# One portion of column copies behind each Relu and each square, in a graph layer on one core

## The chip, the cores and the metric

The kernel runs on one core of one Trainium2 chip. The time is the device time of one execution, in microseconds (us), of the core's whole program. A core has four engines that compute (TensorE or PE, VectorE or DVE, ScalarE or ACT, GpSimd or POOL), and SyncE (SP) beside them, whose queue here issues nearly all the DMAs. Each engine carries out its own list of instructions in order, and the engines wait for each other by semaphores. The kernel's lists are unrolled: there is no loop in the fast path, and an order in the code is an order on the engine.

## The reference: what is computed

A layer of a graph network over 12,500 nodes of 96 features and 412,500 edges (both directions of 200,000 random pairs, and a loop at each node), sorted by target node:

```python
def _mlp(h, W, b, gamma, beta):
    h = jax.nn.relu(h @ W + b)
    mu = jnp.mean(h, axis=0)
    var = jnp.mean(jnp.square(h - mu), axis=0)
    return gamma * (h - mu) * jax.lax.rsqrt(var + EPS) + beta

node_feat = _mlp(x, W_node, ...)                       # 12500 x 96
edge_feat = _mlp(edge_attr, W_edge, ...)               # 412500 x 96, from 4 numbers an edge
message = concatenate([x[src], x[dst], edge_feat])     # 412500 x 288
message = _mlp(message, W_msg, ...)                    # 412500 x 96
agg = segment_sum(message, dst, 12500)
out = layernorm(x + agg + node_feat)                   # over the features
```

The mean and the variance run over all nodes or all edges, in float32. An edge's message is a Relu of three parts: a product of the source's features, one of the target's, one of the edge's features.

## The kernel before, in words

**Before the main loop.** `tables` multiplies x (which lies in SBUF, features on the partitions, in `xp`, the first 96 partitions of `big`) with two thirds of `W_msg`, and writes the rows to two tables in DRAM: `p_tab` by source node, `q_tab` by target node. `edge_norm` then runs over all the edges for the statistics of the edge features: in 26 turns it loads eight blocks of 2048 edges (`ea`), multiplies (L425), applies the Relu on ACT (L429) and takes the statistics on DVE (L431, `estats`). A loop in `fast` steps through it and in each turn also takes two steps of `nodes`, one of `early_rows`, and some of `store`. `nodes` makes the node features into `agg` (L370 to L372), normalises them and adds x (L381, L382; the result goes over x in `xp`), multiplies the result with a centering matrix (L398), and stores it as `y0` in DRAM (L400, L389). At its end it clears `agg` (L406), the place where the messages are summed later. Since x is gone by then, `back` loads it again from DRAM, in 14 DMAs on SP's queue (L498).

**The main loop** runs over 806 groups of 512 edges (four tiles of 128), one group a step `k`; four groups are a block. Source rows of `p_tab` are fetched by POOL, one indirect DMA for 128 rows (`gather`, L215). 116 early groups are fetched before the loop and parked in DRAM (`spill`); the other 690 are late groups, whose rows POOL brings into a ring of 16 groups while the loop runs. `plan` mixes the early blocks into the late ones. One step does, for its group or for neighbouring ones:

- `message(k)`, DVE (L741): h = Relu(z + source rows), where z is a product in PSUM;
- `squared`, ACT (L755): the squares of two groups of h, every second step;
- `moments`, DVE (L761): two additions of such squares to a sum in PSUM (`mixed`), every second step;
- `places_of`, DVE (L749), and `add`, DVE (L804, L805): once a block, which edge belongs to which node of a window, and the block's sums added to `agg`;
- `sums(k-2)`, PE (L785): the sums by node of the group two steps back;
- `edges`, PE (L705), and `prepare`, ACT (L713): half a block of edge features into the PSUM tile `pr`, of which there is one, and its Relu into `left`;
- `linear(k+2)`, PE (L721): z for the group two steps ahead, from `left` and `rhs` (weights and target rows).

**Column copies.** In every second late group, for three of four pairs, the fourth tile's source rows are not gathered by POOL. Its 128 columns of x are copied instead, one by one, from `xp` in SBUF into a tile `xc`, and multiplied by the source weights within `linear` (L726). There are 249 such tiles. A copy moves 96 x 4 bytes from a place that is only known at run time, so its engine first loads the places into registers: a load of numbers (`TENSOR_LOAD`, L644) brings a portion's places at once, and then a register instruction and a copy follow for each column (L655 on DVE, L657 on ACT). Two `Stream`s, one an engine, hand out portions of `AT_A_TIME` = 16 columns; `SHARES` gives ACT the first 64 or 80 columns of a tile and DVE the others. In each step a stream's credit grows by `RATE` times its portions a tile, and portions are issued while it lasts, as long as the tile's use is no more than `AHEAD_BY` steps away. Before a portion's copies stands the load of the portion after it:

```python
val = self.next or places_at(j, lo, hi, self.engine)
...
    self.next = places_at(*self.parts[self.done], self.engine)
columns(j, lo, val, self.engine)
```

On SP and POOL, and in the main loop on PE, DVE and ACT too, the instructions stand as the code writes them; before the loop a scheduler orders PE, DVE and ACT.

## Time and profile before

| | us |
|---|---|
| median of 3 runs (4052.61 to 4059.76) | 4056.29 |
| the profiled execution's own time | 4053.38 |
| its span in the profile | 4051.7 |
| busy: PE / DVE / ACT / POOL | 2504 / 3050 / 2998 / 2851 |
| first message of the main loop | at 708 |
| last gather issued by POOL | at 4002 |

In the profile's rows an engine's name with a q is its queue (ACTq, DVEq): the part that reads instructions and loads registers. Its time is not in the busy time. A group's row gives line, engine, operation, output and input, count, busy time and mean time in ns of one, then the idle time of the engine just before these instructions and what ended most of it; "issue" means that the engine waited for nothing that the profile shows. In rows in order of time, the first number is the start, the second the length from the first start to the last end of the merged instructions, and the bracket the idle time before. In the row of a window the columns are the window, its length, then for PE, weight loads, DVE, ACT and POOL the busy time and count, then the granted clock, the DMA engines' share, and GB/s.

### The profile page before, as it was taken

The numbers are of one execution on the slowest core, as the hardware profiler recorded it, in microseconds if no ns is written. First come the engines' busy times: TensorE is split into PE (matmuls) and PEld (weight loads), VectorE is DVE, ScalarE is ACT, GpSimd is POOL, SyncE is SP. The second block draws the span as 40 slices with busy tenths as digits, with TensorE's granted clock in tenths as the row PEclk, the third lists the DMA queues.
The fourth block names the chain that finished last, engine by engine and source line by source line (L and its number), as shares of the span: only waits on it lengthen the run. The fifth ranks groups of instructions, "written<-read, shape, count | busy, mean of one in ns | idle before, by whom it ended". The sixth has DMA issues, their size and how long they took to land.

```text
span 4051.7 us, 110364 instructions
## 1 busy us (share of the span) xinstructions
PE 2504.0 (62%) x15667; PEld 2145.1 (53%) x15667; DVE 3049.6 (75%) x16338; ACT 2997.5 (74%) x19818; POOL 2851.2 (70%) x2999
## 2 busy tenths in 40 slices
PE   3345554766666666666666666665666666566567
PEld 3012311665565566666556565555655565556557
DVE  2499898777777777777777777777777777777776
ACT  0465674778777787877787778778787777788774
POOL 7776676777766676767767667666776766767765
PEclk7666776778777777777877777878777877777778
DMA  8764574222222222222222222222222222222224
GB/s 222 270 158 109 149 189 101 57 61 60 55 55 47 54 57 57 58 55 59 57 55 57 57 58 46 55 58 56 57 56 56 60 54 57 57 45 66 48 56 122
DMA packets 209657, 314.64 MB, mean 78 GB/s; under 512 B 122822, under 2 KB 129716, under 8 KB 206080
## 3 DMA queue, kind: packets, MB, share of 16 engines
q0 software_dynamic: 95072, 146.22, 17.9%
q1 hardware_dynamic: 100876, 156.32, 12.9%
q10 hardware_dynamic: 12960, 4.93, 0.5%
q14 instruction: 623, 5.10, 0.4%
q8 instruction: 126, 2.06, 0.2%
HBM read 251.14 MB, written 56.09 MB: 76 GB/s over the span
## 4 chain that ended last, share of the span: by engine, by line
ACT 35%; DVE 19%; issue 18%; ACTq 12%; PE 6%; DMA 5%; DVEq 3%; SPq 1%; POOL 0%; POOLq 0%
ACT xc L657 32%; ACTq L644 10%; DVE estats L431 7%; DVE xc L655 5%; DVEq L644 3%; DVE mixed L761 2%; PE z L721 2%; ACTq L657 2%; DVE h L741 2%; ACT left L713 1%; DMA ea<-stack_d 1%; ACT sq L755 1%; PE pr L705 1%; PE pa L785 1%; DMA q_tab<-trow 1%
## 5 line engine op out<-in xcount | busy, mean ns | idle before, releaser
L215 POOL DMA_INDIRECT pg<-p_tab,src x2907 | 2768.2, 952 | 1151.1 <-issue 790.0
L657 ACT ACTIVATE xc<-big 96x4 uint8 x18592 | 1925.9, 190 | 626.1 <-issue 597.3
L655 DVE COPY xc<-big 96x4 uint8 x13280 | 1503.0, 198 | 696.9 <-issue 693.7
L721 PEld LDWEIGHTS z<-rhs,left 128*128 128x128 f32 x6446 | 1126.4, 254 | 219.0 <-DVE h L741 133.6
L721 PE MATMUL z<-rhs,left 128*128 128x96 f32 x6446 | 1159.5, 338 | 89.1 <-DVE h L741 88.2
L705 PE MATMUL pr<-late,we 128*128 128x512 bf16 x690 | 276.7, 493 | 933.0 <-ACT left L713 913.0
L785 PE MATMUL pa<-at,h 128*97 128x80 f32 x6446 | 837.7, 284 | 0.0
L785 PEld LDWEIGHTS pa<-at,h 128*97 128x97 f32 x6446 | 791.8, 205 | 0.2
L705 PEld LDWEIGHTS <-we 128*128 128x128 bf16 x806 | 86.4, 109 | 1097.7 <-issue 1096.9
L761 DVE TENSOR_TENSOR mixed<-mixed,sq 128x384 f32<-128x384 f32 x802 | 449.9, 561 | 16.3 <-ACT sq L755 2.2
L741 DVE CUSTOM_DVE_ANT_0 h<-z,pg 128x384 f32<-128x384 f32 x690 | 381.1, 556 | 76.8 <-PE z L721 52.1
L713 ACT ACTIVATE left<-pr 127x1024 f32<-127x1024 f32 x403 | 403.7, 1002 | 33.9 <-PE pr L705 33.9
L429 ACT ACTIVATE r<-pr 128x1024 f32<-128x1024 f32 x303 | 299.2, 1034 | 131.5 <-PE pr L425 68.6
L431 DVE BATCH_NORM_STATS2 estats<-r 128x6 f32<-128x512 f32 x606 | 361.3, 674 | 15.9 <-ACT r L429 15.9
L755 ACT ACTIVATE sq<-h 128x768 f32<-128x768 f32 x404 | 335.0, 829 | 43.0 <-DVE h L741 40.9
L425 PE MATMUL pr<-ea,wide 128*128 128x512 bf16 x606 | 225.7, 483 | 222.8 <-ACT r L429 111.8
L425 PEld LDWEIGHTS <-wide 128*128 128x128 bf16 x606 | 69.1, 115 | 367.6 <-issue 330.2
L749 DVE TENSOR_TENSOR at<-rel,mixed 128x496 f32<-128x496 bf16 x202 | 135.2, 669 | 6.8
L726 PE MATMUL z<-w_msg,xc 96*128 96x96 f32 x498 | 133.7, 364 | 0.0
L705 PE MATMUL pr<-early,we 128*128 128x512 bf16 x116 | 46.5, 493 | 117.3 <-ACT left L713 117.3
L726 PEld LDWEIGHTS z<-w_msg,xc 96*128 96x128 f32 x498 | 112.2, 277 | 0.0
L215 POOL DMA_INDIRECT pg<-in_x,src_raw x64 | 61.3, 957 | 20.7 <-issue 19.2
(131 smaller groups left out, 794.4 us busy)
## 6 DMA issues: line engine op xcount, KB each, us to landing
pg<-p_tab,src POOLq DMA_INDIRECT x2907
pb<-spill SPq DMA_DIRECT2D x29, 768.0 KB
spill<-pg SPq DMA_DIRECT2D x55, 384.0 KB
ea<-stack_d SPq DMA_DIRECT2D x25, 480.0 KB
stack_d<-y SPq DMA_DIRECT2D x24, 448.0 KB
late<-stack_d SPq DMA_DIRECT2D x57, 180.0 KB
big<-in_xp SPq DMA_DIRECT2D x28, 336.0 KB
rhs<-q_tab SPq DMA_DIRECT2D x202, 46.5 KB
```

Source lines behind the costliest of these rows:

```text
L215: made = [nc.gpsimd.indirect_dma_start(out=pg[:, i, :], out_offset=None, in_=tab[:, :], in_offset=bass.IndirectOffsetOnAxis(ap=idx[:, i:i ...
L431: nc.vector.bn_stats(stats[:, (k - o) % NS, (k - o) // NS, :], r[:, 1 - o, :])
L644: _, val = nc.values_load_multi_w_load_instructions(numbers[q // TURN % 2][:, q % TURN, lo:hi], engines=[engine], min_val=0, max_val=4 * ( ...
L655: nc.vector.tensor_copy(a, b)
L657: nc.scalar.activation(a, b, AF.Copy)
L705: nc.tensor.matmul(prs[s, half][:, i, :], we[:, 2 * half + i, :], block[s], start=True, stop=True)
L713: nc.scalar.activation(x[:C + WN, 2 * half:2 * half + n, :], pr[:C + WN, :n, :], AF.Relu)
L721: nc.tensor.matmul(zb[k % ZB][:, i * C:(i + 1) * C], left[s % 2][:KR, g % BG, i * P:(i + 1) * P], rhs[:KR, s % RB, g % BG, :], start=True, ...
L741: nc.vector._custom_dve(TENSOR_ADD_SAT, out=h[:, :n, :], in0=z, in1=rows[:, :n, :], s0=MOST, s1=0.0)
L755: nc.scalar.activation(sq[:, :m, :n, :], hb[k // 2 % HP][:, k % 2:k % 2 + m, :n, :C], AF.Square)
L761: nc.vector.tensor_tensor(wide_sq, wide_sq, sq[:, i, :, :], op=OP.add)
L785: nc.tensor.matmul(by_place[s % 2][:C + 1, :NW], hb[k // 2 % HP][:r, k % 2, t, :], at[s % AB][:r, i, o + NW * t:o + NW * (t + 1)], start=i ...
```

## The change

- **Portions.** `SHARES` now holds cuts: ACT's portions are columns 0 to 24, 24 to 48 and 48 to 72 of every tile, DVE's 72 to 92, 92 to 112 and 112 to 128. A load of numbers thus brings 24 places on ACT, and 20, 20 and 16 on DVE. `RATE` is 0.335, which with three portions a tile is one portion a step for each engine, and `AHEAD_BY` is 18.
- **Turns.** `squared` stands in even steps and takes the pair of groups before the current one; `prepare` stands in odd steps. `moments` moves to the even steps. `edges` stands in even steps, `transposed` in odd ones.
- **PE.** `linear(k+2)` comes ahead of `edges` in a step.
- **x.** The normalised nodes are written over `agg`, x stays in `xp`, and `back` with its 14 DMAs is gone. `nodes` takes one step a turn of `edge_norm` instead of two. The columns of `agg` past the last node are cleared at the start, since a product reads them.

```diff
-AT_A_TIME = 16
-SHARES = (64, 80, 80)
-AHEAD_BY = 12
-RATE = 0.36
+SHARES = ((0, 24, 48, 72), (72, 92, 112, P))
+AHEAD_BY = 18
+RATE = 0.335
@@ nodes
+        nc.vector.memset(agg[:C, N:], 0.0)
@@
-            x, y = agg[:C, c:c + N // 10], xp[:, c:c + N // 10]
-            nc.vector.scalar_tensor_tensor(y, x, a_n, y, op0=OP.mult, op1=OP.add)
+            y = agg[:C, c:c + N // 10]
+            nc.vector.scalar_tensor_tensor(y, y, a_n, xp[:, c:c + N // 10], op0=OP.mult, op1=OP.add)
@@
-                    nc.tensor.matmul(py[:, g * C:(g + 1) * C], xp[:, (i + o + g) * P:(i + o + g + 1) * P], center,
+                    nc.tensor.matmul(py[:, g * C:(g + 1) * C], agg[:C, (i + o + g) * P:(i + o + g + 1) * P], center,
@@ fast, the turns of edge_norm
-                    for _ in range(2):
-                        next(node, None)
+                    next(node, None)
@@
-                    if i > 14:
-                        for _ in range(min(3, len(homes))):
-                            back(homes.pop(0))
@@ class Stream
-                    self.parts = [(j, o, o + AT_A_TIME) for j in range(len(COPIED)) for o in range(0, P, AT_A_TIME)
-                                  if (o < SHARES[j % len(SHARES)]) == (engine == ET.Activation)]
+                    self.parts = [(j, lo, hi) for j in range(len(COPIED)) for lo, hi in zip(cuts, cuts[1:])]
@@ before the main loop
                 edges(1, 0)
+                prepare(1, 0)
@@ a step of the main loop
-                    if k % 2:
-                        now = squared(k - 1)
+                    if k % 2 == 0 and k >= 2:
+                        now = squared(k - 2)
                         if waiting:
-                            moments(waiting, k == last - 1)
+                            moments(waiting, False)
@@
-                    if g % BG != 3 and s + 1 < len(order):
-                        if g % 2:
-                            edges(s + 1, 1)
-                        else:
-                            prepare(s + 1, g % BG // 2)
-                    if g % BG == 3:
-                        if s + 2 < len(order):
-                            edges(s + 2, 0)
-                    if k % 2 == 0 and k + ZB - 1 < n and order[steps[k + ZB - 1][0]] < RAW:
-                        transposed(k + ZB - 1)
                     if k + ZB - 1 < n:
                         linear(k + ZB - 1)
+                    u = g % BG
+                    if u % 2:
+                        if s + 1 + u // 2 < len(order):
+                            prepare(s + 1 + u // 2, (u // 2 + 1) % 2)
+                    elif s + 1 + u // 2 < len(order):
+                        edges(s + 1 + u // 2, (u // 2 + 1) % 2)
+                    if k % 2 and k + ZB < n and order[steps[k + ZB][0]] < RAW:
+                        transposed(k + ZB)
@@ after the main loop
+                now = squared(last - 2)
+                moments(waiting, True)
+                waiting = now
```

The line numbers of the main loop's instructions fall by about a dozen: L741 becomes L728, L644 becomes L632, L655 and L657 become L643 and L645, L713 becomes L700, L755 L742, L721 L708, L705 L692, L761 L748, L749 L736.

**DVE's list, in the middle of the main loop, before.** ISA with h is the message, `numbers` the load of a portion's places; "..." stands for the rest of a portion's copies.

```order
L749 TENSOR_TENSOR at_4950<-rel,mixed 128x4x4x31
L804 TENSOR_TENSOR total<-pa_4920,total 97x1
L805 ISA
L805 TENSOR_TENSOR agg<-pa_4920,agg 97x79
L644 TENSOR_LOAD numbers_4977
L655 REGISTER_ALU
L655 COPY xc_4974<-big 96x4
...
L644 TENSOR_LOAD numbers_4977
L655 REGISTER_ALU
L655 COPY xc_4974<-big 96x4
...
```

In that step two portions of 16 follow each other, and the second one's load stands straight behind copies. The same place now:

```order
L728 ISA h_4932<-z_4950,pg_76 128x4x96
L736 TENSOR_TENSOR at_4937<-rel,mixed 128x4x4x31
L791 TENSOR_TENSOR total<-pa_4907,total 97x1
L792 ISA
L792 TENSOR_TENSOR agg<-pa_4907,agg 97x79
L632 TENSOR_LOAD numbers_4963
L643 REGISTER_ALU
L643 COPY xc_4957<-big 96x4
...
L728 ISA h_4930<-z_4948,pb 128x4x96
L748 TENSOR_TENSOR mixed<-mixed,sq 128x384 x2
L632 TENSOR_LOAD numbers_4963
```

A message follows after one portion of 20, and the two sums of squares stand in the next step, no longer in that of the places and sums. Over the whole list DVE's loads of numbers stand 332 times behind a message, 150 behind the sums of squares, 188 behind the sums by place, 156 behind copies and 4 elsewhere before; now they stand 193 times behind a message (6 more behind a memset that follows one), 332 behind the sums of squares, 149 behind the sums by place, 66 behind copies, and once at the start.

**ACT's list, before:** `left` is the Relu, `sq` the squares.

```order
L713 ACTIVATE left_4939<-pr 127x1024
L644 TENSOR_LOAD numbers_4977
L657 REGISTER_ALU
L657 ACTIVATE xc_4975<-big 96x4
...
L644 TENSOR_LOAD numbers_4977
L657 REGISTER_ALU
L657 ACTIVATE xc_4975<-big 96x4
...
L755 ACTIVATE sq<-h_4944 128x768
```

And now:

```order
L700 ACTIVATE left_4927<-pr 127x1024
L632 TENSOR_LOAD numbers_4964
L645 REGISTER_ALU
L645 ACTIVATE xc_4960<-big 96x4
...
L742 ACTIVATE sq<-h_4932 128x768
L632 TENSOR_LOAD numbers_4964
L645 REGISTER_ALU
L645 ACTIVATE xc_4961<-big 96x4
...
```

Behind the Relu stood two loads with 16 copies each; now one load with 24 copies stands there. Before, 469 of ACT's 1162 loads stood behind copies, now 66 of 747.

**PE's list, in one step of the loop, before:** `pa` are the sums by node, `z` the message product, `pr` the edge products.

```order
L785 MATMUL pa_4920<-at_4950,h_4944 97x80 x4
L705 LDWEIGHTS we
L705 MATMUL pr<-late_4965,we 128x512
L705 LDWEIGHTS we
L705 MATMUL pr<-late_4965,we 128x512
L721 MATMUL z_4962<-rhs,left_4939 128x96 x4
L726 MATMUL z_4962<-w_msg,xc_4970 128x96
```

And now:

```order
L772 MATMUL pa_4906<-at_4936,h_4930 97x80 x4
L708 MATMUL z_4949<-rhs,left_4927 128x96 x4
L692 LDWEIGHTS we
L692 MATMUL pr<-late_4951,we 128x512
L692 LDWEIGHTS we
L692 MATMUL pr<-late_4951,we 128x512
```

The edge products, which wait for the Relu that empties `pr`, have moved behind the message product of the same step.

10 lines of the change are left out of this document (2 added, 8 removed).

## The prediction

> **What bounds the kernel now.** I read the page first, then the groups by line, the main loop's window, the loads of numbers, and two engines in order of time.
>
> ```profile
> span 4051.7 us, 110364 instructions
> ACT xc L657 32%; ACTq L644 10%; DVE estats L431 7%; DVE xc L655 5%; DVEq L644 3%; DVE mixed L761 2%; PE z L721 2%; ACTq L657 2%; DVE h L741 2%; ACT left L713 1%; DMA ea<-stack_d 1%; ACT sq L755 1%; PE pr L705 1%; PE pa L785 1%; DMA q_tab<-trow 1%
> L215 POOL DMA_INDIRECT pg<-p_tab,src x2907 | 2768.2, 952 | 1151.1 <-issue 790.0
> L657 ACT ACTIVATE xc<-big 96x4 uint8 x18592 | 1925.9, 190 | 626.1 <-issue 597.3
> L655 DVE COPY xc<-big 96x4 uint8 x13280 | 1503.0, 198 | 696.9 <-issue 693.7
> L705 PE MATMUL pr<-late,we 128*128 128x512 bf16 x690 | 276.7, 493 | 933.0 <-ACT left L713 913.0
> L741 DVE CUSTOM_DVE_ANT_0 h<-z,pg 128x384 f32<-128x384 f32 x690 | 381.1, 556 | 76.8 <-PE z L721 52.1
> 700.00:3970.00 3270.00, 2110.60 (x14042) 1932.01 (x14043) 2476.76 (x15444) 2587.89 (x19385) 2309.26 (x2448) 0.77 0.25 56
> ```
>
> The last row is the main loop: 3270 us, in which DVE is busy for 2477 and ACT for 2588. The rest of their time is almost all "issue" before a column copy (597 us on ACT, 694 on DVE). The next fence tells what that is: the loads of numbers, which the busy time does not count (times in ns: least, median, most).
>
> ```profile
> L644 ACTq TENSOR_LOAD <-numbers x1162: 1011/1021/1039, 713.9 to 3965.2; - x194
> L644 DVEq TENSOR_LOAD <-numbers x830: 1094/1099/1120, 715.1 to 3960.6; - x166
> L794 DVEq TENSOR_LOAD <-base_at x26: 535/596/619, 734.3 to 4005.9; - x26
> L811 DVEq TENSOR_LOAD <-flag x1: 567/567/567, 695.8 to 695.8; - x1
> ```
>
> A load of 16 numbers holds the engine's queue for 1.02 us (ACT) or 1.10 us (DVE). Work already handed to the engine runs on beneath it; nothing behind it starts. So both engines are full. DVE waits only 76.8 us for its products z, and the chain runs mostly through ACT because ACT is ahead by about that much. PE's 913 us before the edge products end on ACT's Relu and cost little more than those 76.8 us. How much of a load is seen depends on what stands ahead of it:
>
> ```profile
> 1447.03 0.56 DVE L741 CUSTOM_DVE_ANT_0 h<-z,pg 128x384 f32<-128x384 f32 x1
> 1448.31 1.84 DVE L655 COPY xc<-big 96x4 uint8 x16 [0.73 <-issue]
> 1450.04 0.56 DVE L741 CUSTOM_DVE_ANT_0 h<-z,pg 128x384 f32<-128x384 f32 x1
> 1450.52 1.16 DVE L761 TENSOR_TENSOR mixed<-mixed,sq 128x384 f32<-128x384 f32 x2
> 1452.38 1.76 DVE L655 COPY xc<-big 96x4 uint8 x16 [0.71 <-issue]
> 1458.80 0.67 DVE L749 TENSOR_TENSOR at<-rel,mixed 128x496 f32<-128x496 bf16 x1
> 1459.45 0.23 DVE L805 TENSOR_TENSOR agg<-pa,agg 97x79 f32 x1
> 1460.22 1.76 DVE L655 COPY xc<-big 96x4 uint8 x16 [0.54 <-issue]
> 1463.10 1.76 DVE L655 COPY xc<-big 96x4 uint8 x16 [1.11 <-issue]
> 2400.18 1.63 ACT L657 ACTIVATE xc<-big 96x4 uint8 x16 [0.30 <-issue]
> 2402.76 1.63 ACT L657 ACTIVATE xc<-big 96x4 uint8 x16 [0.95 <-issue]
> 2404.30 1.00 ACT L713 ACTIVATE left<-pr 127x1024 f32<-127x1024 f32 x1
> 2405.38 0.78 ACT L657 ACTIVATE xc<-big 96x4 uint8 x7
> 2407.32 0.84 ACT L755 ACTIVATE sq<-h 128x768 f32<-128x768 f32 x1
> 2408.50 1.63 ACT L657 ACTIVATE xc<-big 96x4 uint8 x16 [0.34 <-issue]
> ```
>
> On DVE, 0.73 us is left open after a message, 0.71 after the two sums of squares (the second waits for the first, and the load for its issue), 0.54 after the sums by place, 1.11 straight after copies. On no path is the DVE load hidden, so any lengthening is seen in full. On ACT a Relu hides 16 numbers, a square leaves 0.34, copies leave 0.95. POOL comes third: 1.25 us a gather, and in the loop it sometimes waits for a slot of the ring.
>
> **The change part by part.**
>
> *Number of copies on DVE.* 249 tiles of 128 columns are copied. ACT goes from 18592 to 249 x 72 = 17928, DVE from 13280 to 249 x 56 = 13944. Sixteen take 1.76 us and the last alone 0.17, so one is (1.76 - 0.17) / 15 = 0.106: **+664 x 0.106 = +70 us** on DVE, and on ACT, by (1.63 - 0.19) / 15 = 0.096, -64 us.
>
> *Number and places of DVE's loads, at the old length.* Counted in the built order, the loads before stand 332 times after a message, 150 after the sums of squares, 188 after the sums by place, 156 after copies: 332 x 0.73 + 150 x 0.71 + 188 x 0.54 + 156 x 1.11 = 624 us (the page's 694 holds short pauses besides). Now it is 199, 332, 149 and 66 (the 199 with six behind a memset): 145 + 236 + 80 + 73 = 534. **-90 us.**
>
> *Length of DVE's loads.* Two of three portions are now 20 numbers, 498 loads in all; no trace shows 20. Rows of L794: its last load has 2 numbers (202 blocks are 25 times 8 and 2) and is the 535; the usual 8 take 596, so 10 ns a number. Yet 16 take 1099, 503 more than 8. This looks like batches of eight with a round trip each; 20 would then need a third, less four numbers: 503 - 40 = 0.46 us more than 16. From below: four more numbers at 10 ns, 0.04. Between: 63 ns a number, the slope from 8 to 16, 0.25. I take 0.46, because 2 to 8 and 8 to 16 cannot lie on one line, and keep 0.04 and 0.50 as ends. **498 x 0.46 = +229 us.**
>
> The Trainium skill (DMA: Bandwidth & Descriptors, "Latency and other measured facts") gives such a load a floor of about 600 ns, which the rows of 1, 2 and 8 numbers bear out, and it says nothing of steps. The skill (Runtime: NRT & Kernel Launch, on who loads registers) also has about 200 ns a register even in bulk, from HBM, which speaks against longer loads: four more would be 0.8 us, 498 x 0.8 = 398, and the whole 4346 us. The trace disagrees for SBUF: 16 numbers would be 3.2 us and are 1.10.
>
> *Slack.* DVE's 76.8 us of waiting goes where DVE becomes the last engine. The new order helps: message products no longer stand behind edge products that wait for a Relu, and squares are of the pair before. I leave 12 us: **-65 us** (bounds 0 and -77). In the loop DVE comes to 70 - 90 + 229 - 65 = **+144 us**.
>
> *ACT.* The longer load, again by a third batch, is 1.02 + 0.50 = 1.52. From a Relu's start to the copies that would be 1.08 + 0.50, from a square's 1.18 + 0.50 (start to start in the rows above), and four steps 2 x (1.58 + 1.68) + 4 x 24 x 0.096 = 15.7 us. DVE's four: twice message and sums of squares (1450.04 to 1452.38, 2.34 us), once a message (1447.03 to 1448.31, 1.28), once message, places and sums (0.48, then 1458.80 to 1460.22: 1.90), plus 4 x 18.7 x 0.106 of copies and four loads' mean lengthening of 2/3 x 0.46 = 0.31: 4.68 + 1.28 + 1.90 + 7.93 + 1.24 = 17.0. ACT's gain is therefore hidden behind DVE; without that cover it would be the time of the third rival.
>
> *POOL and the ring* are unchanged, and slower consumers only make POOL wait more:
>
> ```profile
> 654.76 0.94 POOL L215 DMA_INDIRECT pg<-p_tab,src  x1 [12.65 <-DMA spill<-pg]
> 4001.92 0.94 POOL L215 DMA_INDIRECT pg<-p_tab,src  x1 [0.30 <-issue]
> POOL pg L215 <- DVE h L741: 242.9, 113, 15.6
> ```
>
> Some 2510 gathers at 1.25 us are 3138 us of the 3347 between the first two rows; the floor is about 200 us below now and not touched.
>
> *Nodes and x, before the loop.* Nodes advance one stage a turn instead of two, and x is not overwritten, so 14 loads of it go from SP's queue.
>
> ```profile
> 404.79 1.00 DVE L400 COPY y0s<-pn 128x384 f32<-128x384 f32 x2
> 407.44 0.56 DVE L400 COPY y0s<-pn 128x384 f32<-128x384 f32 x1 [1.65 <-PE pn L398]
> 409.15 0.56 DVE L400 COPY y0s<-pn 128x384 f32<-128x384 f32 x1 [1.15 <-PE pn L398]
> 411.11 14.34 DVE L431 BATCH_NORM_STATS2 estats<-r 128x6 f32<-128x512 f32 x24 [1.40 <-ACT r L429]
> 485.96 71.30 DVE L431 BATCH_NORM_STATS2 estats<-r 128x6 f32<-128x512 f32 x120 [4.87 <-ACT r L429]
> 508.79 1.26 SPq L498 DMA_DIRECT2D big<-in_xp  x3
> ```
>
> DVE's edge statistics set the pace here. Where two stages stand together, DVE waits 1.65 + 1.15 + 1.40 = 4.2 us, some six times, 25 us; with two copies a turn that break has no cause. The instructions that remain are the same (the clearing of agg only moves), and x's transfers are hidden but for gaps like the 4.87. Bounds 0 (if SP's queue, which now carries y0 stores later, breaks it elsewhere) and -34; I take **-20 us**.
>
> *The last steps* gain one square and two sums ahead of the tail: 0.84 + 1.16, put at +2 and within the rounding.
>
> **Sum**: profiled 4053.4 (span 4051.7) + 144 - 20 = **4177 us**. The median shown, 4056.3, is 3 us above the profiled execution, which is inside what I can resolve.
>
> **The rivals.**
>
> 1. *A load lengthens evenly*, 63 ns a number: 498 x 0.25 = 125 in place of 229, so +40 in the loop and 4053 + 40 - 20 = 4073 us. For it: 16 over 8. Against it: 8 over 2.
> 2. *The batch is larger than eight*, 20 and 24 cost as 16 does (faster). Then 20 more us instead of 229, the DVE sum is 70 - 90 + 20 = 0, ACT falls well under DVE (a load of 1.10 instead of 1.52), 55 us of the waits for z go, and 20 before the loop: 3978 us. It decides where the 20-number load is under 1.31 us: there the sum is zero (70 - 90 + 498 d - 65 - 20 = 0 at d = 0.21). For it: only that 16 is all the trace has above 8. Against it: no other size between 2 and 8 costs anything. The skill's floor, read as a flat price, would give this time.
> 3. *Edge products last* become the bound: a Relu waits for edge products, which now stand behind a message product that waits for copied columns. If half of the 403 Relus waited 0.25 us on the slow engine's path, +50: 4227 us. Against it: the columns may be copied up to 18 steps ahead.
> 4. 200 ns a number, 4346 us, as worked out beside the skill's sentence.
>
> **How the numbers follow.** Forecast 0.58 (its own range 4135 to 4220), first rival 0.14, second 0.23, third 0.03, fourth 0.02. The range of 3970 to 4220 leaves out the lower half of the second rival (0.11) and the upper end with the third and fourth (0.09). A measurement of this kernel can tell 0.2%, 8 us, from no change: faster 0.23 + 0.03 of the first rival = 0.26; the same 0.05 of the first rival + 0.02 of the forecast's lower end = 0.07; slower the rest, 0.67.
>
> **What would show it.** The loads of L632 in the profile after: 20 numbers at 1.56 us on DVE and 24 at 1.5 on ACT bear out the third batch; 1.35 the first rival; under 1.2 the second. DVE's issue idle before copies should rise from 694 to about 830, POOL's waiting should rise, ACT should show waits or idle that it has not now, and the loop should begin some 20 us sooner. I am wrong if DVE's loads of 20 are no longer than those of 16, if the chain still runs through ACT, or if the break around y0s stays.

## The result

The changed kernel takes **3992.5 us** (median of four runs, 3975.3 to 3995.0) against 4057.7 for the kernel before: a ratio of 0.983, with a 95% interval of 0.980 to 0.986 (ratios here and below are of mean times). On another chip it was 3992.2 against 4057.2, 0.983 (0.980 to 0.985). The forecast was 4177 us, slower. The profiled execution took 3975.3 us, 78 less than the profiled one before.

These are rows of the changed kernel's page that answer to those of the prediction. The second is the chain: the work followed back from the last instruction, at each step to what released it.

```profile
span 3973.5 us, 109561 instructions
DVE xc L643 15%; DVEq L632 9%; DVE estats L431 9%; DVE mixed L748 8%; ACT xc L645 8%; POOL pg L214 5%; DVE h L728 3%; DMA pg<-p_tab,src 3%; ACTq L632 2%; PE z L708 2%; DVEq L643 1%; ACT sq L742 1%; DMA x<-in_ea 1%; DMA q_tab<-trow 1%; DMA cols<-in_lasts 0%
L214 POOL DMA_INDIRECT pg<-p_tab,src x2907 | 2774.3, 954 | 1066.6 <-issue 762.7
L645 ACT ACTIVATE xc<-big 96x4 uint8 x17928 | 1817.5, 190 | 585.2 <-issue 559.0
L643 DVE COPY xc<-big 96x4 uint8 x13944 | 1564.3, 197 | 673.7 <-issue 624.0
L708 PE MATMUL z<-rhs,left 128*128 128x96 f32 x6446 | 1244.0, 353 | 902.4 <-DVE h L728 888.8
L728 DVE CUSTOM_DVE_ANT_0 h<-z,pg 128x384 f32<-128x384 f32 x690 | 383.0, 555 | 32.3 <-PE z L708 14.7
L692 PE MATMUL pr<-late,we 128*128 128x512 bf16 x515 | 241.0, 531 | 31.1 <-DVE at L736 15.5
L742 ACT ACTIVATE sq<-h 128x768 f32<-128x768 f32 x404 | 335.2, 830 | 91.3 <-DVE h L728 86.3
```

The chain has gone from ACT (32% in its copies before) to DVE, and POOL's gathers have come into it with 5%. DVE's issue time before copies fell from 694 to 624 us, where I had it rise to 830, although each of its copies costs what it did. PE's 913 us of waiting for ACT's Relu are gone; it now waits in front of its message products, 889 us for DVE's messages where it was 88. DVE waits 32 us before its messages instead of 77. The loads of numbers (ns: least, median, most):

```profile
L632 ACTq TENSOR_LOAD <-numbers x747: 1464/1490/1512, 684.3 to 3865.6; - x187
L632 DVEq TENSOR_LOAD <-numbers x747: 1094/1350/1370, 684.4 to 3868.1; - x187
L781 DVEq TENSOR_LOAD <-base_at x26: 541/596/605, 714.9 to 3928.9; - x26
```

The median of DVE's loads is one of 20 numbers: 1.350 us, 0.25 over the 1.099 of 16, where I had 0.46. Where the loop begins, in order of time, before and after:

```profile
708.06 0.56 DVE L741 CUSTOM_DVE_ANT_0 h<-z,pg 128x384 f32<-128x384 f32 x1 [7.60 <-PE z L721]
```

```profile
681.12 0.56 DVE L728 CUSTOM_DVE_ANT_0 h<-z,pg 128x384 f32<-128x384 f32 x1 [7.56 <-PE z L708]
```

The first message comes 27 us sooner. From there to its last copy DVE took 3259 us before and 3193 now, 66 less; from that copy to the end it is 84 and 100 us, 15 more. -27 - 66 + 15 = -78 is the difference of the two profiled executions.

I added up DVE's list between the first message and the last copy in the two traces, from the start of each instruction to the start of the next, by what follows what (us; in brackets the count and mean). A load is in the step from the instruction ahead of it to the first copy behind it:

```
                                   before            after         undone sums    turns alone
copy to copy of one portion        1394              1473          1474           1394
load behind a message              430 (332, 1.30)   286 (193)     479 (334)      194 (150)
load behind sums of squares        192 (150, 1.28)   484 (332)     286 (191)      424 (332)
load behind the sums by place      159 (188, 0.85)   100 (149,0.67) 151 (149,1.01)  94 (188,0.50)
load behind copies                 204 (156)          85 (66)       86 (66)       203 (156)
on to `at` of places_of            118 (196, 0.60)    92 (195,0.47) 116 (194,0.60)  92 (196,0.47)
message behind message or squares  107                28            26             58
all else                           655               645           647            786
whole list                        3259              3193          3265           3245
```

"Undone sums" and "turns alone" are two experiments below. The copies cost 79 more, as forecast (70). The loads, for which I had 139 more, cost 30 **less**. `at` costs 26 less, a term that my sum did not have.

The place in the program where this happens, in order of time, first before, then after, each with the load that stands behind `at` in DVE's list:

```profile
1511.77 0.56 DVE L741 CUSTOM_DVE_ANT_0 h<-z,pg 128x384 f32<-128x384 f32 x1
1512.25 1.16 DVE L761 TENSOR_TENSOR mixed<-mixed,sq 128x384 f32<-128x384 f32 x2
1513.44 0.67 DVE L749 TENSOR_TENSOR at<-rel,mixed 128x496 f32<-128x496 bf16 x1
1514.10 0.23 DVE L805 TENSOR_TENSOR agg<-pa,agg 97x79 f32 x1
1514.86 0.28 DVE L655 COPY xc<-big 96x4 uint8 x2 [0.53 <-issue]
```

```profile
L644 DVEq TENSOR_LOAD <-numbers x1: 1098/1098/1098, 1513.6 to 1513.6; - x1
```

```profile
1523.47 0.56 DVE L728 CUSTOM_DVE_ANT_0 h<-z,pg 128x384 f32<-128x384 f32 x1
1523.94 0.66 DVE L736 TENSOR_TENSOR at<-rel,mixed 128x496 f32<-128x496 bf16 x1
1524.59 0.23 DVE L792 TENSOR_TENSOR agg<-pa,agg 97x79 f32 x1
1524.97 1.13 DVE L643 COPY xc<-big 96x4 uint8 x10 [0.16 <-issue]
```

```profile
L632 DVEq TENSOR_LOAD <-numbers x1: 1097/1097/1097, 1523.7 to 1523.7; - x1
```

`at` reads the node numbers from the same PSUM tile, `mixed`, to which the sums of squares are added. Before, the sums stood right ahead of it: `at` waited for the second to end (1512.25 + 1.16 = 1513.41), and with `at` the queue waited, so the load, four instructions further on in the list, began at 1513.6, after `at` had started. Now the sums stand in another step. The queue goes past `at` while the message still runs, and the load begins at 1523.7, before `at` starts at 1523.94. Both loads bring 16 numbers; the pause in front of the copies is 0.16 instead of 0.53 us.

The end of the program has a price that the trace before did not show. Here are the last products (the layer's output), before, in the profiled execution after, and in the second profile of the changed kernel; below the last is its window of 55 us at the end:

```profile
L1070 PE MATMUL py<-dm,agg x196: 275/275/350, 4014.5 to 4036.4; 97*128 97x96 f32 x196
```

```profile
L1059 PE MATMUL py<-dm,agg x196: 275/275/350, 3938.0 to 3959.9; 97*128 97x96 f32 x196
```

```profile
L1059 PE MATMUL py<-dm,agg x196: 421/421/529, 3939.3 to 3981.1; 97*128 97x96 f32 x196
```

```profile
3936.70:3991.70 55.00, 44.42 (x203) 43.47 (x201) 25.83 (x42) 14.25 (x26) 16.04 (x11) 0.50 0.34 90
```

At a granted clock of 0.50 a product takes 421 ns instead of 275 and the 196 of them 42 us instead of 22. From the last copy to the end the two profiles differ by 17 us, which fits the two groups in which the changed kernel's times lie, 3975 to 3979 and 3991 to 3995; the times of `sums_in_odd_3` below lie in two groups as well, 4049 to 4051 and 4064 to 4069, each some 73 us above its counterpart.

Three of the five sets of runs below ran on chips on which the kernel before took 5831 to 5945 us, 1.44 to 1.47 times as long; their totals are told, called disturbed, but decide nothing here. What is different there is seen in the register instructions of ACT's column copies, first in the kernel before, then with only the part on x changed on such a chip (ns: least, median, most):

```profile
L657 ACTq ALU_OP  x18592: 35/35/53, 716.0 to 3969.5; - x200
```

```profile
L646 ACTq ALU_OP  x18592: 3/35/1397, 986.8 to 5742.9; - x200
```

Of the 18592 on ACT, 1162 took 0.6 to 0.9 us there, and half as many on DVE; some six in ten of DVE's overlap one on ACT. The medians of loads of 8 and more numbers, and of the steps of DVE's list that are compared below, are the same on such chips to 0.01 us.

### The profile page after: what moved, and what is told of

Same layout as the page of the kernel before. It is cut to its first block, busy times and chain, and to the rows that moved or that the text cites. A ratio compares the mean times of both kernels' runs of the same rounds, so it can differ in the third digit from the quotient of the medians.

```text
span 3973.5 us, 109561 instructions
## 1 busy us (share of the span) xinstructions
PE 2642.1 (66%) x15447; PEld 2273.6 (57%) x15667; DVE 3080.1 (78%) x17003; ACT 2903.0 (73%) x19154; POOL 2859.8 (72%) x2999
## 4 chain that ended last, share of the span: by engine, by line
DVE 39%; issue 23%; DVEq 10%; ACT 10%; DMA 6%; POOL 5%; PE 3%; ACTq 3%; SPq 0%; POOLq 0%; another core or an unknown queue 0%
DVE xc L643 15%; DVEq L632 9%; DVE estats L431 9%; DVE mixed L748 8%; ACT xc L645 8%; POOL pg L214 5%; DVE h L728 3%; DMA pg<-p_tab,src 3%; ACTq L632 2%; PE z L708 2%; DVEq L643 1%; ACT sq L742 1%; DMA x<-in_ea 1%; DMA q_tab<-trow 1%; DMA cols<-in_lasts 0%
## 5 line engine op out<-in xcount | busy, mean ns | idle before, releaser
L645 ACT ACTIVATE xc<-big 96x4 uint8 x17928 | 1817.5, 190 | 585.2 <-issue 559.0
L643 DVE COPY xc<-big 96x4 uint8 x13944 | 1564.3, 197 | 673.7 <-issue 624.0
L708 PE MATMUL z<-rhs,left 128*128 128x96 f32 x6446 | 1244.0, 353 | 902.4 <-DVE h L728 888.8
L708 PEld LDWEIGHTS z<-rhs,left 128*128 128x128 f32 x6446 | 1107.1, 258 | 988.1 <-DVE h L728 973.0
L772 PEld LDWEIGHTS pa<-at,h 128*97 128x97 f32 x6446 | 899.4, 219 | 132.0 <-issue 66.3
L772 PE MATMUL pa<-at,h 128*97 128x80 f32 x6446 | 903.2, 299 | 34.5 <-issue 26.9
L700 ACT ACTIVATE left<-pr 127x1024 f32<-127x1024 f32 x403 | 404.7, 1004 | 78.7 <-PE pr L692 45.7
L748 DVE TENSOR_TENSOR mixed<-mixed,sq 128x384 f32<-128x384 f32 x802 | 449.9, 561 | 15.7 <-ACT sq L742 1.8
L728 DVE CUSTOM_DVE_ANT_0 h<-z,pg 128x384 f32<-128x384 f32 x690 | 383.0, 555 | 32.3 <-PE z L708 14.7
L742 ACT ACTIVATE sq<-h 128x768 f32<-128x768 f32 x404 | 335.2, 830 | 91.3 <-DVE h L728 86.3
L692 PE MATMUL pr<-late,we 128*128 128x512 bf16 x515 | 241.0, 531 | 31.1 <-DVE at L736 15.5
L692 PEld LDWEIGHTS <-we 128*128 128x128 bf16 x806 | 117.8, 149 | 39.2 <-issue 35.4
L736 DVE TENSOR_TENSOR at<-rel,mixed 128x496 f32<-128x496 bf16 x202 | 133.1, 659 | 0.0
L713 PE MATMUL z<-w_msg,xc 96*128 96x96 f32 x498 | 116.9, 324 | 0.0
L713 PEld LDWEIGHTS z<-w_msg,xc 96*128 96x128 f32 x498 | 97.0, 241 | 0.0
L398 PEld LDWEIGHTS pn<-center,agg 96*128 96x128 f32 x196 | 41.4, 271 | 31.9 <-DVE y0s L400 22.1
```

What stands on the lines that cost most here:

```text
L643: nc.vector.tensor_copy(a, b)
L645: nc.scalar.activation(a, b, AF.Copy)
L692: nc.tensor.matmul(prs[s, half][:, i, :], we[:, 2 * half + i, :], block[s], start=True, stop=True)
L700: nc.scalar.activation(x[:C + WN, 2 * half:2 * half + n, :], pr[:C + WN, :n, :], AF.Relu)
L708: nc.tensor.matmul(zb[k % ZB][:, i * C:(i + 1) * C], left[s % 2][:KR, g % BG, i * P:(i + 1) * P], rhs[:KR, s % RB, g % BG, :], start=True, ...
L728: nc.vector._custom_dve(TENSOR_ADD_SAT, out=h[:, :n, :], in0=z, in1=rows[:, :n, :], s0=MOST, s1=0.0)
```

## Experiments

The account to be tested (theory A): the time is DVE's list plus what lies ahead of it, and the list became shorter because `at` and the load behind it no longer wait for the sums of squares. Rival B: the gain is TensorE's new order. Rival C: it is the time ahead of the loop.

### The sums of squares back in front of the sum by place

Only the two sums move; squares, Relus and products keep their turns. (Two lines that start and end the loop follow suit and are left out here.)

```diff
-                        now = squared(k - 2)
-                        if waiting:
-                            moments(waiting, False)
-                        waiting = now
+                        waiting, now = now, squared(k - 2)
+                    if k % 2 and k >= 5:
+                        moments(waiting, False)
```

> The changed kernel with one thing undone: the sums of the squares (two on DVE for two messages) go back to the odd steps, where the sum by place that reads the same PSUM tile stands right behind them; squares, left sides and products keep their turns. Theory A: the sum by place waits for the squares' sums again (0.60 us instead of 0.47, 194 times, 25 us) and the load behind it starts later (0.98 us instead of 0.67, 149 times, 46 us), so 71 us more, 4063 us (4040 to 4075): all of the change's gain is gone. Rival B: the products still stand ahead of the edge products, so nothing changes, 3992 us (within 10). Rival C: nothing changes.

> The same kernel as sums_in_odd, run again: in the first set the kernel before itself took 5831 us, with over a thousand register instructions of 0.7 us on ACT, of which its profile at 4053 us has none, so that set's totals say little of the loop that was predicted. If the kernel before takes about 4057 us here: theory A (the sum by place waits for the sums of squares again, 25 us, and the load behind the sums by place starts later, 46 us): 71 us over the changed kernel, 4063 us, 4040 to 4075, so a ratio of 0.995 to 1.005. Rival B (TensorE's order) and rival C (the time ahead of the loop): 3992 us, a ratio of 0.984. If it takes 5800 us again: the transitions' medians decide, 0.60 us from the squares' sum to the sum by place and 1.02 from the agg to the load behind it, as in the first set.

> The changed kernel with the sums of squares back in the odd steps, ahead of the sum by place, on a chip on which, it is hoped, the kernel before takes 4057 us as when it was predicted. Theory A: 25 us (194 sums by place wait 0.13 us longer) and 46 us (149 loads behind the sums by place start 0.31 us later) over the changed kernel's 3992 us: 4063 us, 4040 to 4075, a ratio of 0.996 to 1.004 to the kernel before. Rival B (TensorE's order) and rival C (the time ahead of the loop): 3992 us, 0.984.

Measured undisturbed (sums_in_odd_3): **4064.1 us**, a ratio of 1.0006 (0.9991 to 1.0021). The whole gain is gone. Its list is the third column of the table: 3265 us, 72 over the changed kernel's, 24 of it at `at`, 51 at the load behind the sums by place. The place in order of time, and the load:

```profile
1502.21 0.56 DVE L728 CUSTOM_DVE_ANT_0 h<-z,pg 128x384 f32<-128x384 f32 x1
1502.68 1.16 DVE L748 TENSOR_TENSOR mixed<-mixed,sq 128x384 f32<-128x384 f32 x2
1503.88 0.67 DVE L736 TENSOR_TENSOR at<-rel,mixed 128x496 f32<-128x496 bf16 x1
1504.53 0.23 DVE L792 TENSOR_TENSOR agg<-pa,agg 97x79 f32 x1
1505.57 0.80 DVE L643 COPY xc<-big 96x4 uint8 x5 [0.81 <-issue]
```

```profile
L632 DVEq TENSOR_LOAD <-numbers x1: 1353/1353/1353, 1504.1 to 1504.1; - x1
```

The load of 20 begins behind `at` again, and 0.81 us of it is seen. Theory A's 4063 us holds; B and C, at 3992, fall as explanations of the whole. That one undone part costs the whole gain doesn't make it the only part: the others are still in this kernel, those that shorten it and those that lengthen it (more copies on DVE, longer loads), and together they come to about nothing. In the disturbed sets the ratios were 0.956 and 0.954, with medians of 0.60 us on to `at` and 1.02 behind the sums by place, as here.

### The changed kernel again, beside the kernel before

> The changed kernel itself, beside the kernel before on the same chip: where the kernel before takes 5800 to 5950 us, as in the two sets so far, nothing says yet what the change is worth there. Theory A (DVE's list): the list of the copying part is shortened by the sums by place standing free of the sums of squares, 71 us, also there, so the changed kernel stands about 71 us below sums_in_odd, a ratio of 0.940 to 0.945 to the kernel before against sums_in_odd's 0.954 to 0.956, unless the 0.7 us register instructions hide DVE's list altogether: then 0.954 to 0.956. If the kernel before takes 4057 us: 0.983 again.

3992.2 us, 0.983 (0.980 to 0.985): the set ran undisturbed, and the result stands. Its DVE list is 3193 us, to 0.1 us that of the first profile; it is 17 us longer in the tail, at the clock of 0.50.

### Message products behind edge products again

```diff
-                    if k + ZB - 1 < n:
-                        linear(k + ZB - 1)
                     u = g % BG
@@ behind edges, prepare and transposed
+                    if k + ZB - 1 < n:
+                        linear(k + ZB - 1)
```

> The changed kernel with the message products of a step put behind its edge products, transposes and copies of left sides again; all else as changed. Theory A: DVE's list keeps its length, the edge products wait for ACT's left sides again (their idle time ahead on TensorE rises from 31 us towards 933) and hold z back, so DVE's waits for z rise from 32 us towards the 77 us of before: 10 to 45 us more than the changed kernel, 4015 us. Rival B: this order is the whole gain, so 65 us more, 4057 us. Rival C: nothing, 3992 us. (If the kernel before takes 5800 us here, the ratio to the other kernels of this set and the idle time before z and before the edge products decide.)

> The changed kernel with message products behind the edge products again, on such a chip. Theory A: DVE's list keeps its length and only its waits for z rise, from 32 us towards the 77 us of before: 10 to 45 us over the changed kernel, 4002 to 4037 us, a ratio of 0.986 to 0.995. Rival B: the whole gain goes, 4057 us, 1.00. Rival C: nothing, 0.983.

Measured undisturbed (edges_first_2): **4002.3 us**, 0.986 (0.985 to 0.988), 10 us over the changed kernel.

```profile
L692 PE MATMUL pr<-late,we 128*128 128x512 bf16 x515 | 242.2, 533 | 320.2 <-ACT left L700 301.5
L728 DVE CUSTOM_DVE_ANT_0 h<-z,pg 128x384 f32<-128x384 f32 x690 | 382.6, 555 | 36.0 <-PE z L708 22.6
```

The edge products wait for ACT's Relu again, 320 us against 31, and DVE still waits only 36 us against 32. A's sum holds at its lower end; the order on PE (rival B) is worth 10 us of the gain. In a disturbed set: 0.956.

### The turns alone

The kernel before with squares and their sums in even steps, Relus in odd ones, and message products first; the loads, shares and x as before.

> The kernel before with the turns alone: squares and their sums in even steps, the left sides in odd ones, message products ahead of edge products; loads of 16 numbers as before. Theory A: DVE's list falls to about 3109 us (196 x 0.13 us less ahead of the sums by place, 188 x 0.35 us less behind them, 44 messages behind messages without their wait), 150 us less, but ACT's list, with its shares as before, has 3226 us of work without any wait, 42 us less than its 3268 us before, so ACT decides and the time falls by 30 to 50 us, to 4008 to 4028 us. Rival B (the order on TensorE and the waits for z that it ends are the whole gain): 65 us less or more, 3992 us. Rival C: no change, 4057 us.

> The same kernel as turns, run again for the same reason as sums_in_odd_2. If the kernel before takes about 4057 us here: theory A: DVE's list falls by 150 us, but ACT's 3226 us of work without a wait decide: 30 to 50 us less than before, 4017 us, a ratio of 0.988 to 0.993, with ACT hardly waiting and DVE waiting over 100 us. Rival B: 3992 us or less, 0.984 or lower. Rival C: 4057 us, 1.00.

> The kernel before with the turns and the products' order alone, on such a chip. Theory A: DVE's list is 150 us shorter, but ACT's list, which keeps its 16-number loads and its share, has 3226 us of work and now decides: 30 to 50 us less than before, 4007 to 4027 us, a ratio of 0.988 to 0.993. Rival B: 0.984 or lower. Rival C: 1.00.

Measured undisturbed (turns_3): **4046.5 us**, 0.998 (0.997 to 0.999), 9 us less, where I expected 30 to 50. The chain, and by groups ACT's Relus and squares, DVE's sums of squares and messages; below them ACT's two groups in the kernel before:

```profile
ACT xc L657 39%; ACTq L644 13%; DVE estats L431 7%; ACTq L657 2%; ACT left L713 2%; PE z L721 1%; DVE xc L655 1%; PE pa L785 1%; DMA q_tab<-trow 1%; DMA ea<-stack_d 1%; DVEq L644 1%; DMA late<-stack_d 1%; PE pr L705 1%; DVE mixed L761 1%; DMA x<-in_ea 0%
```

```profile
L713 ACT ACTIVATE left<-pr 127x1024 f32<-127x1024 f32 x403 | 404.4, 1004 | 75.0 <-PE pr L705 63.5 <-PE z L721 11.0
L755 ACT ACTIVATE sq<-h 128x768 f32<-128x768 f32 x404 | 333.6, 826 | 5.7 <-DVE h L741 4.6 <-POOL squares L775 0.4
L761 DVE TENSOR_TENSOR mixed<-mixed,sq 128x384 f32<-128x384 f32 x802 | 450.4, 562 | 161.4 <-ACT sq L755 146.9
L741 DVE CUSTOM_DVE_ANT_0 h<-z,pg 128x384 f32<-128x384 f32 x690 | 379.9, 555 | 28.4 <-PE z L721 25.3 <-PE z L726 1.8 <-issue 1.1
```

```profile
L713 ACT ACTIVATE left<-pr 127x1024 f32<-127x1024 f32 x403 | 403.7, 1002 | 33.9 <-PE pr L705 33.9
L755 ACT ACTIVATE sq<-h 128x768 f32<-128x768 f32 x404 | 335.0, 829 | 43.0 <-DVE h L741 40.9
```

ACT decides, as A said: 39% of the chain in its copies, and DVE's gain (the fourth column: 65 us behind the sums by place, 26 at `at`, 49 before messages) comes back as 147 us of waiting for ACT's squares. But ACT's list, from its first Relu to its last copy, fell by 8 us (3268 to 3260) and not by 42: the 43 us that its squares waited for messages before are 6 now, while its Relus wait 75 us instead of 34 for edge products. I had counted ACT's work without the waits that the new order would give it.

So the rest of the change matters: with the larger portions, fewer columns on ACT and x kept, ACT's copies fall from 39% of the chain to 8%. From turns_3 to the changed kernel it is 54 us. By the profiles (the second one of the changed kernel), DVE's list falls by 52 us, which I put down to the portions without a run that shows it, the loop starts 27 us sooner, and the time from the last copy to the end rises from 90 to 117 us: 52 + 27 - 27 = 52.

### x in SBUF alone, the portions alone, the two parts without the portions

> The kernel before with one part of the change alone: x stays in SBUF (no reload of xp, one portion of the node pass a step). Theory A (the time is DVE's list of the copying part plus what lies ahead of it): the first message came at 708.1 us before and at 681.1 us after, and only this part can have moved it, so 27 us less, 4030 us (20 to 30 less), with DVE's list of the copying part unchanged at about 3259 us. Rival C (the gain is nearly all from the time ahead of the loop, since a queue with less on it lets the gathers run earlier throughout): 65 us less, 3992 us. Rival B (the gain is from TensorE's order, message products ahead of edge products): between 0 and 27 us less.

> The kernel before with x kept in SBUF alone, on a chip on which, it is hoped, the kernel before takes 4057 us. Theory A: the 27 us by which the first message came earlier, 4030 us (4027 to 4037), a ratio of 0.993 to 0.995. Rival C (the time ahead of the loop is the whole gain): 3992 us, 0.984.

> The kernel before with the portions alone: loads of 24 numbers on ACT and of 20, 20 and 16 on DVE, 72 rows to 56, and the two pacing constants. Theory A: DVE's list by the measured means of its transitions, 334 loads behind messages at 1.296 + 0.167 us, 191 behind squares at 1.281 + 0.167, 149 behind the sums by place at 0.845 + 0.14, copies 1473 instead of 1394 us, comes to 3315 us instead of 3259, so 56 us more, 4114 us; if ACT, which now has slack, lets the products come earlier, the waits for z between two messages (53 us over their bare time) go and it is 3 us more, 4061 us. So never below the kernel before by more than measuring error. Rival B: all of the loads' price and none of the gain, 56 us more. Rival C: 0. A price of the loads by batches of eight (0.46 us for a third batch), as forecast: some 105 us more than the 56, 4220 us.

> The kernel before with the portions alone (loads of 24 numbers on ACT, 20, 20 and 16 on DVE, 72 rows to 56), on such a chip. Theory A: DVE's list is that of sums_in_odd_3, 3265 us, 27 us later for want of the part with x, and with up to 53 us of waits for z between two messages: 4091 us to 4144 us, 4100 us, slower than before, a ratio of 1.008 to 1.021. A rival by which the larger loads pay by themselves, as ACT is relieved: below 1.00.

> The changed kernel with the portions of before (loads of 16, shares of 64, 80 and 80 rows on ACT, the two pacing constants). Theory A: turns_3 less the 27 us of x_stays: 4019 us (4012 to 4026), a ratio of 0.989 to 0.993, since ACT's list decides; so the portions, which cost 35 us or more alone, are worth 27 us here. A rival by which the portions are worth nothing and the turns with x give all: 3992 us, 0.984.

All five ran in disturbed sets: ratios of 0.997 and 0.998 for x, 0.967 and 0.968 for the portions, 0.979 for x with turns (the turns alone 0.986 and 0.980 there). On such a chip larger portions pay by themselves; the prediction was not for such a chip, and the stalls of the register instructions, which lie on both engines, are not explained by anything measured here. What the portions alone do where the kernel before takes 4057 us stays open; by the lists it should not be faster, since its medians are those of the undone sums (0.60 us on to `at`, 1.02 behind the sums by place).

### Loads of 4 to 28 numbers

```diff
-SHARES = ((0, 24, 48, 72), (72, 92, 112, P))
+SHARES = ((0, 4, 12, 24, 48, 72), (72, 76, 84, 100, P))
```

> The changed kernel with loads of 4, 8, 16 and 28 numbers on DVE and of 4, 8, 12, 24 and 24 on ACT, the same rows on each. By a line with a floor (0.094 + 0.063 us a number on DVE, 0.08 + 0.059 on ACT, not under 0.53): DVE 0.53 to 0.57, 0.60, 1.10 and 1.85 us, ACT 0.5 to 0.55, 0.55, 0.78 and 1.49. By batches of eight (0.596 for the first, 0.5 for each next): DVE 0.60, 0.60, 1.10 and 2.1, ACT 0.55, 0.55, 1.02 and 1.49. The kernel: per tile 0.3 us more of loads and 0.19 us for one more of them on DVE, 249 times, 122 us more than the changed kernel, 4115 us (4070 to 4130).

A tile's four loads on DVE, of 4, 8, 16 and 28 numbers, and a tile's five on ACT (4, 8, 12, 24 and 24, as least, median and most):

```profile
L632 DVEq TENSOR_LOAD <-numbers x1: 343/343/343, 3450.0 to 3450.0; - x1
L632 DVEq TENSOR_LOAD <-numbers x1: 595/595/595, 3454.6 to 3454.6; - x1
L632 DVEq TENSOR_LOAD <-numbers x1: 1098/1098/1098, 3455.7 to 3455.7; - x1
L632 DVEq TENSOR_LOAD <-numbers x1: 1850/1850/1850, 3457.7 to 3457.7; - x1
L632 ACTq TENSOR_LOAD <-numbers x5: 309/783/1492, 3081.3 to 3089.6; - x5
```

(1850 - 343) / 24 = 63 ns a number on DVE, and 343 - 4 x 63 = 91 ns beside it; 8, 16 and 20 lie on that line (0.595, 1.097, 1.351). On ACT it is 59 ns and 75. The medians over all 249 tiles say the same (0.345, 0.597, 1.098 and 1.849 us on DVE). Single loads stray on this disturbed chip, those of four most: 53 of 249 on DVE took about 0.7 us, and 53 under 0.1. It is a line, with neither batches nor a floor down to 4 numbers: the expectation by a line with a floor is wrong at 4, that by batches of eight at 4, at 28 and, on ACT, at 12. The set was disturbed, so its total (5910 us, 0.995 of before) isn't weighed.

### More tiles gathered by POOL

If DVE's list is the bound, a copied tile less is worth 9 to 10 us to it and costs POOL one gather of 1.25. Three versions, all of the changed kernel:

```diff
-COPIED = [q for q in range(RING // 2, LP - 6) if q % TURN != TURN - 1]
+... if q % TURN != TURN - 1 and q % 20 != 10]        # fewer16
+... if q % 8 not in (1, 3, 7)]                       # fewer41
+... if q % TURN != TURN - 1 and q % 16 != 1]         # fewer21
@@ fewer21, in ahead_of: the slot is cleared again before the next copied tile
+            if g % 2 and not without:
+                zeroed.discard(q % len(ring))
```

> The changed kernel with about one in twenty more of the ring's tiles gathered by POOL as rows instead of being copied by ACT and DVE (the numbers are loaded for 16 or so tiles fewer, and POOL issues as many more gathers). Theory A (DVE's list is the bound): per tile left out DVE saves 56 copies x 0.106 + loads of 3.8 us = 9.7 us, 150 us in all; then POOL's gathers become the bound, 2526 x 1.2515 us from 633.7 us on and 47 us behind the last: about 3845 us if they never wait, 3850 to 3890 with some waits, a ratio of 0.949 to 0.959. A rival by which POOL's gathers already decide (they are 5% of the chain that ended last): each added gather costs its 1.25 us, 20 us more than the changed kernel, 4012 us. Rival B (the order on TensorE): no change, 3992 us.

> The changed kernel with one more of every eight of the ring's tiles gathered by POOL as rows (q % 8 == 1): 207 copied tiles instead of 249, 42 gathers more. Nothing is left out. If the kernel before takes 4057 us: theory A (DVE's list is the bound): DVE's list falls by 42 x 9.7 us, 400 us, under POOL's 633.7 + 2552 x 1.2515 + 47 = 3875 us, so POOL decides: 3875 to 3910 us, a ratio of 0.955 to 0.964. A rival by which POOL decides already: 42 x 1.25 = 53 us more than the changed kernel, 4045 us. If it takes 5800 us: the register instructions of 0.7 us come with the copies, one sixth of which are gone, so one sixth of the 1500 us by which that set is slower goes too, 250 us, and the ratio to the kernel before is about 0.91.

> The changed kernel with one more of every sixteen of the ring's tiles gathered by POOL (q % 16 == 1), 21 tiles, and the slot set to zero by DVE before its next copied tile, 20 times. Nothing is left out. Theory A: DVE's list falls by 21 x 9.7 = 204 us and rises by 20 x 0.2 = 4 us, POOL's floor is 633.7 + 2531 x 1.2515 + 47 = 3848 us and decides: 3850 to 3880 us, 10 to 35 us under the 3889 us of the version with 42 tiles fewer, a ratio of 0.949 to 0.957. A rival: with DVE's and POOL's lists now near each other (3770 and 3848 us), each waits for the other in places, and it is 3889 us or more.

fewer16 leaves old rows in a ring slot that a later message adds, so it computes other messages than the layer's; it ran disturbed, 0.963. **fewer41: 3888.6 us**, 0.959 (0.957 to 0.960). **fewer21: 3859.3 us, 0.949 (0.947 to 0.951)**, the best kernel of the study, 3.3% under the changed one. POOL's waits on DVE's messages (us in total, times, longest), after and in fewer21:

```profile
POOL pg L214 <- DVE h L728: 175.6, 100, 8.6
```

```profile
POOL pg L214 <- DVE h L730: 19.8, 65, 0.3
```

POOL waits for nearly nothing now and is the bound, as A said, at 3859 against an estimated 3848 us: from 635.5 us to its last gather at 3794.0 none starts more than 1.3 us behind the one before it, and DVE's last copy is over at 3707.9. DVE's list is 168 us shorter than in the changed kernel, 8 us a tile. With 42 tiles fewer DVE has time left over, waiting for gathers:

```profile
L728 DVE CUSTOM_DVE_ANT_0 h<-z,pg 128x384 f32<-128x384 f32 x690 | 380.7, 554 | 260.0 <-DMA pg<-p_tab,src 226.2 <-PE z L708 21.9 <-PE z L713 9.0
```

## Why the prediction was wrong

- **What bounds the kernel** was read rightly: both engines full, ACT ahead by little. In turns_3 some 140 us off three of DVE's entries gave 9 us, since ACT was the bound. That DVE becomes the bound and ACT's gain is hidden came true (the chain above; ACT's squares wait 86 us for DVE now).
- **Number of copies on DVE**: +70 forecast, +79 measured.
- **Length of DVE's loads is the step that failed first.** +229 us stood on a third batch of 0.46 us; the load is a line of 63 ns a number and the term is 498 x 0.25 = 125, 104 us less. I set the line aside for two rows, the loads of one number (0.567) and of two (0.535). They are dearer than the load of four (0.343), so they aren't on the line of the others; why is open, but two odd rows should not have outweighed 8 against 16. The first rival had the right price and a chance of 0.14. ACT's sign (24 numbers at 1.5 us) came true and told nothing: the line gives 1.49 there too. The Trainium skill's floor of about 600 ns (DMA: Bandwidth & Descriptors, "Latency and other measured facts"), which I cited beside it, does not hold here: 4 numbers take 0.31 to 0.34 us.
- **Number and places of DVE's loads, at the old length, is where the sign went wrong.** I priced a load by the instruction ahead of it and took 0.54 us for the sums by place from the old order. I saw that `moments` moved and did not ask what else reads its tile. By the order without the sums in front, that pause is 0.16 us for 16 numbers. In all, number and places came to -155 us at the old length (the loads' -30 less the 125 of length), where I had -90; 51 of these 65 us are this pause. With the wait of `at`, a term that I left out, this is 51 + 26 = 77 us on the list; undoing it alone costs 72 us (sums_in_odd_3). Price and places together: 104 + 77 = 181 of the 210 us between my +144 and the measured -66. The rest is waits (below) and 14 us of smaller differences in the loads, against 9 us more of copies.
- **Slack**: -65 forecast for the waits for z. On the list, messages behind a message or the sums of squares come 79 us cheaper and smaller entries 10 us. The first reason I gave, the products' order, is not it: with the old order in edges_first_2 DVE waits 36 us for its messages, against 77 before. Nor is it that DVE is the bound: in turns_3 ACT is, and DVE waits 28 us. What the kernels with few such waits share is the new turns of squares, their sums and Relus, the second reason I gave; which of the three does it was not tried.
- **Nodes and x**: -20 forecast, the first message came 27 us sooner. That x stays was not timed alone on an undisturbed chip.
- **The last steps**: put at +2; the end is 15 us later behind the last copy in the profiled execution and 32 in the second profile. The loop now ends ahead of POOL: the last gather was issued 35 us behind the last copy before (4001.9 against 3967.4) and 52 us behind it after (3926.1 against 3873.9; the row is below). Behind the last copy DVE's messages wait 11.6 us for those rows, where they waited for none before, and PE's sums by node wait for the messages; the granted clock falls to 0.50 at 3920.4 us, before the last 196 products. That the one brings the other is argued, not tried. I called POOL's floor untouched, 200 us below, and did not ask what its lateness does to the last stage. I also had POOL's waiting rise; for DVE's messages it fell from 243 to 176 us.

```profile
3926.10 0.95 POOL L214 DMA_INDIRECT pg<-p_tab,src  x1 [0.30 <-issue]
```

- **The rivals**: the second's 3978 us lies near the result, but its mechanism (20 numbers cost as 16 do) is refuted: right time for the wrong reason. The first's 4073 us is 81 over the result; the wait behind the sums of squares, which no rival had, is 77. The third is not borne out: ACT's Relus wait 79 us instead of 34, but the chain runs through DVE (in turns_3, where ACT is the bound, such waits did cost time). The fourth's 200 ns a number would be 4 us for 20, which took 1.35.

## What to carry to other kernels

When an instruction is moved, list everything that reads or writes its tiles, not only what it computes: here two additions that had moved were worth 72 us because an unrelated instruction read another part of their tile, and the queue's wait for it kept back a load behind it. Where an engine's queue ran ahead here, it hid part of a load; the pause seen behind an instruction belongs to the order it was seen in and cannot be carried over. And when two engines share a bound, ask what a third could take more cheaply: 21 tiles handed to POOL gave twice what the whole change gave.

## What the runs showed of the hardware

- A load of numbers from SBUF into registers took 0.09 + 0.063 us a number on DVE's queue, from 4 to 28 numbers, and 0.075 + 0.059 on ACT's, from 4 to 24, while loads of one or two on DVE took 0.54 to 0.57.
- An instruction that waited for a semaphore held back the load behind it in its engine's queue (begun at 1513.6 us, `at` at 1513.44); where it did not have to wait, the load began before it (1523.7 against 1523.94).
- In the changed kernel's second profile the granted clock stayed at 0.50 from 3922.9 us to the end although 196 products ran one behind another for 42 us; in the first profile, by the trace's record of the clock, it was at full speed again from 3937.5 to 3961.4, behind 4.6 us of products in a row. The Trainium skill (TensorE: Matmul & The Clock Gate, "Part 1: The HAM clock gate") has the clock rise after about 3.4 us of sustained work. The first trace fits that, the second does not.
- In three of the five sets the kernel before took 1.44 to 1.47 times as long, with register instructions of up to 1.4 us on ACT and DVE; the cause was not found.
